# A planner's transfer time that grows with the bytes under way in front, in a four-layer graph network kernel

## The chip, the cores and the metric

The kernel runs on one core of one Trainium2 chip. The metric is the device time of one execution in microseconds (us), as the median of several runs; lower is better. The core has TensorE (matmuls; the profile shows them as PE, and the loading of their weights as PEld), VectorE (DVE), ScalarE (ACT), GpSimd (POOL) and SyncE (SP), which issues nearly all transfers here. The engines run side by side, each takes its instructions strictly in the order in which they were built, and they wait for each other through semaphores.

## The reference

Sixteen graphs of 1024 nodes with 128 features pass through four residual layers. `adj` is a sparse symmetric pattern with random weights, about 16 entries in a row.

```python
h = relu(layernorm(x)); x = x + L0(h, adj)   # relu([h, (adj^T h) / degree] W^T + b)
h = relu(layernorm(x)); x = x + L1(h, adj)   # leaky_relu((adj / degree) h W^T + b)
h = relu(layernorm(x)); x = x + L2(h, adj)   # two rounds of edge scores, see below
h = relu(layernorm(x)); x = x + L3(h, adj)   # attention over adj's entries: softmax((Wh1 + Wh2^T) * (adj + I)) Wh, elu
# L2, each of two rounds l:
score[n, m] = sigmoid(we2 . relu(a[n] + b[m] + be1) + be2)      # a, b: x times the halves of We1
msg = (adj * score) @ x
x = layernorm(x + relu([x, msg] Wu1 + bu1) Wu2 + bu2) * gamma + beta
```

## The kernel before

**Stages and lanes.** Three generators of work are woven by `weave` (L1630): `main` of graph b (both rounds of layer 2), `last` of graph b - 1 (end of layer 2, layer 3) and `first` of graph b + 1 (layers 0 and 1, then `build`). They belong to the lanes `m`, `c` and `a`, with buffers and PSUM banks of their own; lane `a` has a single bank while all three run. What repeats is one graph, about 290 us.

**Layer 2 on the sparse entries.** A graph's adjacency is cut in 128 x 128 tiles. `build` makes of each tile short lists of its entries: `pr`/`rank`, `on`, `onT`, `omT`, `om` are made one after another through lane `a`'s single bank, by TensorE matmuls (`pr`, `pn`, `pq`, `pm`) that ScalarE or VectorE read out at once. `twice` (L1116) copies `on` to `st` by four small transfers. `split` (L1211) turns the projected features (`bb` in PSUM) into two half-precision parts, `part`, and four transfers put them in a second arrangement, `both`. In a round, `gather` adds for each list the terms of both ends in PSUM (`pre`: two matmuls with `part`, two with `both`), `hid` is its relu, `dots` gives the scores `sc`, `scores` spreads them as `val`, `scatter` puts them back on the tile's grid (`p`, partly with 64-column matmuls), `upd` multiplies with the adjacency that `load_adj` fetched as `adj`, and `messages` sums `msg`.

**Between the rounds.** `between` (L1523) runs for each half of the nodes: it loads the transposed features `xm` by `self.back(xT, oldT)` (L1006), scales the messages into the same tile, and computes `h2` (TensorE row `h`, L594), `xn`, `tx` and the layer norm; it transposes the result (`tp`, read out as `xfT`), stores it (`xTk`), and calls `split` for the second round. The second round's first `pre` needs the first half's `both`.

**Layers 0 and 1.** `first` loads each row tile of `adj` twice (`at`, `ct`, 512 KB each), transposes it (`tn`), and stores it in `adjT`. `layer1` (L572) loads strips `l` of `adjT` (512 KB) into three row buffers, so that strip t waits until the matmuls `nb` of strip t - 3 are done. Layer 3 loads strips `a` (384 or 256 KB) into one buffer, each after VectorE's last use of the strip before.

**What sets the order.** All instructions are recorded first. `Issue` (L67) then plans them and fixes each engine's order by `settle` (L286), which ties neighbours in the plan together. `links` finds what an operation needs; `costs` (L131) gives each operation the time that its engine is busy and the time until its result is there (`late`); `walk` (L194) is a list scheduler: forward it goes through time, and at each point starts on the queue that can go first the ready operation of the best rank; it also keeps count of buffers and of at most eight transfers under way. `order` (L271) takes a first forward walk, then three times a backward walk, whose times give the ranks, and a forward walk with these ranks; it keeps the plan that ends first. All transfers but some of the weights' stand on SP's queue. A change of the matmul's form (float32 to other, 64 columns to full) costs the plan `SWITCH_NS`.

In `walk`, a transfer starts when the eighth before it has landed, and lands after its `late`, whatever else is under way.

Of the kernel before, what the change touches and what calls it, by code (L numbers as in the profile page):

```python
# [59 lines left out]
SIGNAL_NS = 45.0  # L60
RESULT_NS = {"PE": 163.0, "Activation": 120.0, "DVE": 88.0, "Pool": 80.0}
SWITCH_NS = 60.0
DMA_NS, DMA_NS_PER_BYTE, DMAS = 1900.0, 5.2e-3, 8
PASSES = 3


class Issue:  # L67
# [63 lines left out]
    def costs(self):  # L131


        self.busy, self.late, self.form = [], [], []
        for op, queue, kind in zip(self.ops, self.queue, self.kind):
            out, form = op.outs[0].bass_ap, (False, False)
            n, late = self.size(op.outs[0]), RESULT_NS.get(queue, 0.0)
            aps = [a.bass_ap for a in op.ins if hasattr(a, "bass_ap")]
            psum = bool(aps) and aps[0].space == bass.MemoryType.PSUM
            if kind == "Matmult":  # L140
                n = self.size(op.ins[0])
                form = op.ins[0].dtype == F32, out.shape[0] < 128
                if form[0]:
                    busy = max(n / 1.2 + 6, 112) * (1 if op.is_transpose else 2)
                else:
                    busy = 32 if form[1] else max(n / 2.4 + 2.5, 25)
            elif kind == "DMACopy":
                size = n * WIDTH[op.outs[0].dtype] * out.shape[0]
                inside = all(a.space == bass.MemoryType.SB for a in (out, aps[0]))
                busy = 630 if inside else 470  # L150
                late = DMA_NS + size * DMA_NS_PER_BYTE - busy
            elif queue == "Activation":
                busy = n / 1.2 + (50 if psum else 92) + 92 * (len(aps) - 1)
            elif queue == "DVE":
                wide = [a for a in aps if a.size() > 128]
                fast = kind == "TensorScalarPtr" and len(wide) == 1 and not psum
                if kind in ("BNStats", "TensorReduce"):
                    n = self.size(op.ins[0])
                busy = n * (0.53 if fast else 1.0625) + 55 + 64 * (len(aps) > len(wide))
            else:  # L160
                busy = 1560
            self.busy.append(busy)
            self.late.append(busy + late)
            self.form.append(form)
# [29 lines left out]
    def walk(self, rank, seq, back=False):  # L194


        n, queues = len(self.ops), sorted(set(self.queue))
        edges, others = (self.front, self.after) if back else (self.after, self.front)
        waits = [len(v) for v in others]
        users, turn, homes = self.turns(seq)  # L200
        given, parked, live, over = dict.fromkeys(homes, 0), {}, {}, {}
        ready, start, line = [0.0] * n, [0.0] * n, {q: [] for q in queues}
        soon, now = {q: [] for q in queues}, {q: [] for q in queues}
        free, landed, sent, was = dict.fromkeys(queues, 0.0), [0.0] * DMAS, 0, (False, False)

        def offer(j):

            new = {}
            for name in self.uses[j]:
                if name in turn and name not in live:  # L210
                    new.setdefault(self.tiles[name].tag, set()).add(turn[name])
                else:
                    ready[j] = max(ready[j], live.get(name, 0.0))
            for tag, mine in new.items():
                at = given[tag]
                while at in mine:
                    at += 1
                if at <= max(mine) or len(homes[tag]) < len(mine):
                    key = at + 1 if at <= max(mine) else given[tag]
                    parked.setdefault((tag, key), []).append(j)  # L220
                    return
                ready[j] = max(ready[j], sorted(homes[tag])[len(mine) - 1])
            heappush(soon[self.queue[j]], (ready[j], rank[j], j))

        for j in range(n):
            if not waits[j]:
                offer(j)
        for _ in range(n):
            at, q = min(
                (free[q] if now[q] else max(free[q], soon[q][0][0]), q)  # L230
                for q in queues if now[q] or soon[q]
            )
            while soon[q] and soon[q][0][0] <= at:
                heappush(now[q], heappop(soon[q])[1:])
            j = heappop(now[q])[1]
            if self.kind[j] == "DMACopy" and not back:
                at = max(at, landed[sent % DMAS])
                landed[sent % DMAS] = at + self.late[j]
                sent += 1
            elif q == "PE":  # L240
                at += SWITCH_NS * self.switched(j, was, back)
                was = self.form[j]
            start[j], free[q] = at, at + self.busy[j]
            line[q].append(j)
            end = at + (self.busy[j] if back else self.late[j] + SIGNAL_NS)
            freed = {}
            for name in self.uses[j]:
                users[name] -= 1
                over[name] = max(over.get(name, 0.0), end)
                if name not in turn:  # L250
                    continue
                tag = self.tiles[name].tag
                if name not in live:
                    live[name] = heappop(homes[tag])
                    freed.setdefault(tag, []).append(given[tag] + 1)
                    given[tag] += 1
                if not users[name]:
                    heappush(homes[tag], over[name])
                    freed.setdefault(tag, []).append(given[tag])
            for tag, keys in freed.items():  # L260
                for key in dict.fromkeys(keys):
                    for k in parked.pop((tag, key), ()):
                        offer(k)
            for k, lag in edges[j]:
                ready[k] = max(ready[k], at + lag)
                waits[k] -= 1
                if not waits[k]:
                    offer(k)
        return start, line
# [1545 lines left out]
```

## Time and profile before

| | |
|---|---|
| median of 3 runs | 4826.11 us (4824.32 to 4826.47) |
| the profiled execution | 4815.52 us |
| its span, first to last instruction | 4813.6 us |
| mean granted TensorE clock | 0.975 of full |
| transfers issued on SP | 4,418, of which 2,304 of 11 or 16 KB |
| moved | 618.15 MB, mean 128 GB/s |

The profile is one execution. A group's line reads: source line, engine, operation, output and inputs with their shapes, count, then busy time in us, mean ns of one, and the idle time of its engine just before such instructions with what ended most of it. A line of waits gives who waited for what: total us, times, longest. A line of transfers gives the count, the size of one and the median us from issue to landing. A timeline's line gives start, length and, in brackets, the idle time before it and what ended it. Names are without buffer numbers.

### The profile page before, as it was taken

The page shows a single profiled execution, that of the slowest core. Times are in us where ns is not written, and L with a number is a line of the kernel's source. Part 1 is how long each engine was busy: PE and PEld are TensorE (multiplying, and loading weights), DVE is VectorE, ACT ScalarE, POOL GpSimd, SP SyncE. Part 2 cuts the span into 40 slices and gives each one's busy share as a digit, 9 for nine tenths or more (in the row PEclk, how much of TensorE's full clock was granted, in tenths as well). Part 3 has the DMA queues.
Part 4 walks back from the last instruction along what each step waited for, and adds up shares of the span by engine and source line. Part 5 has one row for each costly group of instructions (what it writes and reads, how often), then busy time and mean ns, then how long its engine had stood idle before and what let it go on. Part 6 is the DMA issues. An engine that isn't in the chain of part 4 may idle for free.

```text
span 4813.6 us, 133882 instructions
## 1 busy us (share of the span) xinstructions
PE 4428.3 (92%) x53685; PEld 3601.4 (75%) x53685; DVE 3881.1 (81%) x9128; ACT 2982.1 (62%) x7238; POOL 175.2 (4%) x137
## 2 busy tenths in 40 slices
PE   6997999999999999999999999999999999999986
PEld 5776777777787777777777787777877777777765
DVE  3875797897978879797897978879797886978877
ACT  4756576575766657566575765757566575765643
POOL 0000000000000000000000000000000000000000
PEclk8997999999999999999999999999999999999997
DMA  7362535436354453635436354453535536354321
GB/s 208 79 186 69 161 100 159 122 91 197 83 170 113 129 162 86 180 96 155 133 85 191 95 162 122 114 173 93 173 102 149 141 85 181 99 158 122 81 74 57
DMA packets 945031, 618.15 MB, mean 128 GB/s; under 512 B 220688, under 2 KB 874768, under 8 KB 944400
## 3 DMA queue, kind: packets, MB, share of 16 engines
q1 hardware_dynamic: 939296, 607.87, 44.1%
q8 instruction: 423, 6.93, 0.6%
q10 hardware_dynamic: 5104, 1.65, 0.1%
q14 instruction: 208, 1.70, 0.1%
HBM read 446.44 MB, written 100.66 MB: 114 GB/s over the span
## 4 chain that ended last, share of the span: by engine, by line
PE 42%; DVE 25%; DMA 14%; ACT 10%; SPq 4%; issue 4%; POOL 0%; DVEq 0%; ACTq 0%; POOLq 0%
PE pre L1343 6%; DVE hid L1365 5%; PE p L1486 5%; PE nb L540 5%; DVE val L1441 4%; DMA at<-in_adj_dram 4%; PE msg L436 4%; PE sc L1389 4%; PE pre L1349 3%; PE h L594 3%; PE bb L548 2%; SPq L1123 2%; PE hp L436 2%; ACT hid L1364 2%; DMA both<-part 2%
## 5 line engine op out<-in xcount | busy, mean ns | idle before, releaser
L1365 DVE SCALAR_TENSOR_TENSOR hid<-pre,hid 128x320 f16<-128x320 f32 (+1 forms) x2048 | 996.4, 508 | 192.5 <-ACT hid L1364 184.8
L1364 ACT ACTIVATE hid<-pre 128x320 f16<-128x320 f32 (+1 forms) x2048 | 890.6, 458 | 365.4 <-PE pre L1349 355.5
L1343 PE MATMUL pre<-om,part 128*128 128x320 fp8e4 (+1 forms) x4096 | 968.6, 309 | 21.7 <-DVE hid L1365 9.8
L1349 PE MATMUL pre<-st,both 128*128 128x176 fp8e4 (+1 forms) x4096 | 692.0, 245 | 47.4 <-DMA both<-part 46.0
L1441 DVE TENSOR_TENSOR val<-onT,u 128x1024 f32<-128x1024 fp8e4 x576 | 697.8, 1220 | 3.3
L436 PE MATMUL msg<-upd,xf 128*128 128x128 f32 (+3 forms) x3008 | 648.6, 328 | 9.8 <-DVE upd L1493 9.8
L1349 PEld LDWEIGHTS <-both 128*128 128x128 f16 x4096 | 389.4, 98 | 208.0 <-issue 62.9
L1389 PE MATMUL sc<-slide,hid 128*128 128x1 f16 x12800 | 431.8, 163 | 19.1 <-DVE hid L1365 17.8
L436 PEld LDWEIGHTS msg<-upd,xf 128*128 128x128 f32 x3008 | 420.7, 191 | 30.0 <-DVE upd L1493 13.0
L1389 PEld LDWEIGHTS <-hid 128*128 128x128 f16 x12800 | 405.6, 96 | 49.8 <-DVE hid L1365 33.5
L1204 ACT ACTIVATE om<-pm 128x320 fp8e4<-128x320 f32 (+1 forms) x576 | 268.8, 467 | 231.5 <-PE pm L1150 225.7
L1486 PE MATMUL p<-val,omT 128*128 128x64 f16 (+1 forms) x6528 | 391.4, 204 | 16.7 <-DVE val L1441 15.1
L1410 ACT ACTIVATE tan<-sc,be_s,down 128x8 f32<-128x8 f32 (+1 forms) x960 | 296.4, 356 | 170.3 <-PE sc L1389 160.1
L1343 PEld LDWEIGHTS <-part 128*128 128x128 f16 x4096 | 345.8, 98 | 72.6 <-issue 45.3
L1493 DVE SCALAR_TENSOR_TENSOR upd<-p,adj 128x512 f32<-128x512 f32 x512 | 351.7, 687 | 28.8 <-PE p L1486 27.4
L1486 PEld LDWEIGHTS <-omT 128*128 128x128 fp8e4 x6528 | 337.4, 97 | 40.4 <-issue 25.1
L436 PE MATMUL hp<-wh,e 128*128 128x129 f32 x2048 | 323.8, 287 | 14.1 <-DVE e L768 13.9
L1107 ACT ACTIVATE far<-iota_off,mid 128x384 f16<-128x384 f16 x448 | 279.0, 627 | 56.6 <-DVE on L1111 45.5
L1197 DVE TENSOR_TENSOR omT<-pq,odd_off 128x384 fp8e4<-128x384 f32 x448 | 248.0, 554 | 64.0 <-PE pq L1193 62.0
L594 PE MATMUL h<-xm,wu_sb 128*128 128x512 f32 x512 | 274.3, 637 | 27.2 <-DMA xm<-xT 23.8
L1189 ACT ACTIVATE onT<-pn 128x256 fp8e4<-128x256 f32 (+1 forms) x576 | 250.7, 435 | 66.2 <-PE pn L1135 60.4
L436 PEld LDWEIGHTS hp<-wh,e 128*128 128x128 f32 x2048 | 273.2, 196 | 21.5 <-DVE e L768 17.2
(224 smaller groups left out, 7841.3 us busy)
## 6 DMA issues: line engine op xcount, KB each, us to landing
at<-in_adj_dram SPq DMA_DIRECT2D x128, 512.0 KB, 5.4
ct<-in_adj_dram SPq DMA_DIRECT2D x128, 512.0 KB, 5.4
adjT<-tn SPq DMA_DIRECT2D x128, 512.0 KB, 6.3
l<-adjT SPq DMA_DIRECT2D x128, 512.0 KB, 4.9
adj<-adjT SPq DMA_DIRECT2D x256, 256.0 KB, 3.5
a<-adjT SPq DMA_DIRECT2D x128, 384.0 KB, 3.7
both<-part SPq DMA_DIRECT2D x256, 128.0 KB, 2.3
adj<-adjT SPq DMA_DIRECT2D x448, 64.0 KB, 2.6
```

The source lines that it names most:

```text
L436: nc.tensor.matmul(dst, left, right, start=opened is None, stop=True, skip_group_check=True)
L594: nc.tensor.matmul(ps, wu1_sb[:, l, i, kb * P : (kb + 1) * P], src, start=(i == 0), stop=(i == 1),)
L1107: nc.scalar.activation(far[:, :n], self.iota[t == u][:, :n], AF.Abs, bias=s.mid[:, i : i + 1])
L1343: nc.tensor.matmul(pre[:, :c], parts[:, k, u % Q, 1 - d], om, start=(k == 0), stop=True, skip_group_check=True,)
L1349: ins = nc.tensor.matmul(pre[:, at : at + n], both[:, k, t % Q, d], st[:, k * n : (k + 1) * n], start=False, stop=True, skip_group_check=True,
L1364: nc.scalar.activation(hid[:, 0, :c], pre[:, :c], AF.Relu)
L1365: nc.vector.scalar_tensor_tensor(hid[:, 1, :c], pre[:, :c], 0.0, hid[:, 0, :c], op0=OP.max, op1=OP.subtract)
L1389: nc.tensor.matmul(sc[:, k, g : g + 1], self.hid[self.done + g][:, v, at : at + P], sign, start=(g, v, k) == (*order[0], 0), stop=True, sk ...
L1410: nc.scalar.activation(dst, src, AF.Tanh, bias=path.be2[:, self.l : self.l + 1], scale=path.down[:, self.l : self.l + 1],)
L1441: nc.vector.tensor_tensor(val, onT[:, i : i + each].rearrange("p i (c n) -> p i c n", n=n), v.rearrange("p k i o -> p i k o").to_broadcast ...
L1486: nc.tensor.matmul(dst, left, right, start=n < first, stop=True, skip_group_check=True)
L1493: nc.vector.scalar_tensor_tensor(upd, ps, S_SCALE, self.adj[:, d * Q : (d + 1) * Q], op0=OP.add, op1=OP.mult,)
```

## The change

A transfer's time in the plan had been 1900 ns plus 0.0052 ns for each byte. Now it is 1900 ns plus 0.0039 ns for each byte, plus 0.0033 ns for each byte that is still under way at its issue: of each of the last eight transfers, the share that has not landed, taken as linear in time. The added time counts for the landing (so for the limit of eight), for the release of buffers and for the operations that wait for the data. It is in the forward walk alone; the backward walk, which ranks, has each transfer's own time. No computation and no transfer is changed; the order of the instructions on the engines is what can differ.

```diff
-DMA_NS, DMA_NS_PER_BYTE, DMAS = 1900.0, 5.2e-3, 8
+DMA_NS, DMA_NS_PER_BYTE, DMA_NS_BEHIND, DMAS = 1900.0, 3.9e-3, 3.3e-3, 8
...
-        self.busy, self.late, self.form = [], [], []
+        self.busy, self.late, self.form, self.bytes = [], [], [], []
...
-            n, late = self.size(op.outs[0]), RESULT_NS.get(queue, 0.0)
+            n, late, size = self.size(op.outs[0]), RESULT_NS.get(queue, 0.0), 0
...
+            self.bytes.append(size)
...
-        free, landed, sent, was = dict.fromkeys(queues, 0.0), [0.0] * DMAS, 0, (False, False)
+        free, sent, was = dict.fromkeys(queues, 0.0), [(0.0, 0.0, 0)] * DMAS, (False, False)
...
+            more = 0.0
             if self.kind[j] == "DMACopy" and not back:
-                at = max(at, landed[sent % DMAS])
-                landed[sent % DMAS] = at + self.late[j]
-                sent += 1
+                at = max(at, sent[0][1])
+                more = DMA_NS_BEHIND * sum(
+                    n * (end - at) / (end - then) for then, end, n in sent if end > at
+                )
+                sent = sent[1:] + [(at, at + self.late[j] + more, self.bytes[j])]
...
-            end = at + (self.busy[j] if back else self.late[j] + SIGNAL_NS)
+            end = at + (self.busy[j] if back else self.late[j] + more + SIGNAL_NS)
...
-                ready[k] = max(ready[k], at + lag)
+                ready[k] = max(ready[k], at + lag + more * (lag > 0.0))
```

## The prediction

> **What bounds the kernel now.** I read the page from the top: busy time of each engine, then the costliest groups, then the time to landing of each transfer, then who waited for whom on TensorE, then the same for the SP queue, and last the timeline of one batch round the two largest waits that a transfer ends.
>
> ```profile
> PE 4428.3 (92%) x53685; PEld 3601.4 (75%) x53685; DVE 3881.1 (81%) x9128; ACT 2982.1 (62%) x7238; POOL 175.2 (4%) x137
> ...
> L1486 PE MATMUL p<-omT,val 128*64 128x128 fp8e4 x5376 | 238.0, 224 | 14.2 <-DVE upd L1493 13.9
> ```
>
> TensorE is the bound: its matmul row stands idle for 4813.6 - 4428.3 = 385 us. Batches 5 to 9 (1450 to 2900 us) idle 87 us, or 17 us in each batch of 290. So at most some 8% is to be won, and only what changes TensorE's own waits or its own work counts. The second line is kept for later: matmuls on a 64-column share of the array.
>
> ```profile
> at<-in_adj_dram SPq DMA_DIRECT2D x128, 512.0 KB, 5.4
> adjT<-tn SPq DMA_DIRECT2D x128, 512.0 KB, 6.3
> both<-part SPq DMA_DIRECT2D x256, 128.0 KB, 2.3
> st<-on SPq DMA_DIRECT2D x1792, 11.0 KB, 1.8
> xm<-xT SPq DMA_DIRECT2D x32, 256.0 KB, 5.2
> xm<-xTk SPq DMA_DIRECT2D x32, 256.0 KB, 3.3
> ```
>
> Two rows of 256 KB, one landing in 5.2 us and one in 3.3: size alone doesn't set the time. The old formula (1900 ns + 0.0052 ns a byte) gives 3.26 us for both. I fitted all SP transfers of this trace to their own bytes and to the bytes under way at their issue: 1859 ns + 0.00387 ns a byte + 0.00329 ns a byte in front. The old formula is off by 1.05 us rms and 0.48 us short on average, the new one by 0.55 us and 0.05. So the new planner sees transfers about as they are.
>
> ```profile
> PE pre L1349 <- DMA both<-part: 46.0, 46, 2.4
> PE pm L1150 <- DVE omT L1197: 24.6, 42, 1.3
> PE h L594 <- DMA xm<-xT: 23.8, 14, 2.7
> PE tn L1035 <- ACT tn L1036: 17.7, 28, 1.7
> PE tn L1035 <- DVE own L565: 12.3, 13, 1.9
> PE tn L1035 <- DMA at<-in_adj_dram: 10.5, 19, 1.4
> ```
>
> The columns are total us, times, longest. Where matmul and weight-load row are idle together, the xm wait counts 18.8 us and the both wait 30.1 us; 22.5 of the latter fall on one place, the first `pre` of the second round, 14 times at 1.6 us. The xm wait is also one place in each batch, 1.7 us. These are the waits that a better guess of landing times can remove.
>
> ```profile
> 1439.26 0.36 SPq L972 DMA_DIRECT2D l<-adjT  x1
> 1439.67 0.57 SPq L1006 DMA_DIRECT2D xm<-xT  x1
> ...
> 1442.54 1.06 PE L540 MATMUL nb<-z,l 128*128 128x128 f32 x8
> 1446.23 1.10 PE L594 MATMUL h<-xm,wu_sb 128*128 128x512 f32 x2 [2.63 <-DMA xm<-xT]
> ...
> 1452.87 0.59 SPq L1228 DMA_DIRECT2D both<-part  x1
> ...
> 1457.55 0.49 PE L1349 MATMUL pre<-st,both 128*128 128x256 fp8e4 x3 [2.27 <-DMA both<-part]
> ```
>
> The xm load is issued right behind a 512 KB strip l, which itself waits until `nb` of three strips before frees its row (at 1439.2); it lands after 6.4 us. The old planner put 4.8 us of matmuls between that `nb` and the `h` that reads xm. Needed: 0.4 (issue of l) + 6.4 + 0.1 = 6.9 us. The wait is the planner's error.
>
> **What the Trainium skill says.** "DMA: Bandwidth & Descriptors", section "Queues, rings and completion order": each DMA engine takes a ring's descriptors in order, so a transfer stands behind the bytes issued before it. The trace agrees (5.2 against 3.3 us above). The same page, "Anatomy of one DMA", fits about 2.0 us + bytes/436e3, which is 3.2 us for 512 KB; here such loads take 5.4, and the measurement decides. "TensorEngine Tiling (Array Packing)", "Key Properties": changing the tiling mode drains TensorE. The trace agrees: by the starts of neighbouring matmuls without a wait, the one before a run of 64-column matmuls takes 90 ns more than usual, and the last of the run 156 ns against 29 within it. A run costs 90 + 127 = 217 ns over its matmuls; the planner counts 60. "Perfetto Trace Analysis", "Identifying the Most-Contended Engine", warns that matmul busy time is no measure of headroom; so I count waits and changed work, not busy shares.
>
> **The change, part by part.** No instruction is added or removed; each engine gets the same ones in another order (POOL's is the same). The backward pass, which ranks, has only the shorter own time (512 KB: 4.6 us before, 3.9 now), so loads rank as less urgent, while the forward pass sees them land later. What comes of both stands in the two built orders; I compare these, and price the matmuls between two places by the mean distance of such matmuls in this trace.
>
> 1. The xm load. Between the freeing `nb` and `h` there are now 30 matmuls instead of 20, worth 7.6 us instead of 4.8; a strip load `a`, which waits for VectorE, no longer stands in front of it on SP. 7.6 covers 6.9. Gain: the 18.8 us in which both rows were idle, nearly all: -19.
> 2. both, second round, first half. From the last `bb` to the first `pre` that reads it: 5.6 us of matmuls before, 7.0 now. Needed by the sample above: 1457.55 - 1449.94 (end of that `bb`) = 7.6; by the mean wait (5.6 + 1.6) 7.2. A 384 KB `a` load moves from ahead of it to behind it. Left over 0.2 us x 14 = 3 of 22.5: -19.
> 3. The other `both` places: first round 5.1 us of cover to 5.7, second half 4.7 to 7.2. Their waits are 6.6 us ended by the DMA and about 5 shown as issue; gain -8.
> 4. The transposes `tn` of the adjacency tiles: `at` now has some 1.5 us more work in front of it. Counting for every read-out by ScalarE or VectorE how far the matmuls up to the next reader, or to the next user of its single PSUM bank, fall short of its duration, `tn` goes from 47 to 26 us. The sum of this count over all read-outs is 299 us before, and the trace has 308 us of idle time ended by ScalarE and VectorE: the count has the right size. I take -15 of the 21, since the three wait rows hold only 40 us.
> 5. The builder's single bank by the same count: `om` 85 to 90, `onT` 52 to 66, `rank` 12 to 20, `omT` 53 to 36: +11. `xfT` 8 to 14, `hT` +2.5, `upd` -4, the layer outputs -5: together +10.
> 6. Narrow runs. The order splits the 5,376 narrow matmuls into 528 runs instead of 428. 100 x 217 ns = +22. Float32 to other changes go from 2,026 to 2,038 at 4 ns each: nothing.
> 7. SP's queue. It has no spare order: a strip load `a` blocks it while it waits for VectorE, up to 34.7 us at a time (440 us in all). Loads of `a` move behind xm and both, the copies `st` and loads `adj` change places with them; nine in ten of those keep over 10 us of matmuls as cover, against 1.8 to 4.5 us of landing. New waits are not shown by the trace: bound from 0 to 20 us (one of 1.4 us per batch, like those removed), nearer the bottom: +6. Below nothing isn't likely, since all named gains are counted.
>
> Sum: -19 - 19 - 8 - 15 + 10 + 22 + 6 = -23. Start and end of the program (57 us idle in the first 290, 72 in the last 464) keep their chains. The profiled execution took 4815.5 us (span 4813.6), the median of the runs is 4826.1, 10.6 more; against its own time this makes 4792, against the median 4803. Since every removed wait brings the next one nearer, I take some 3 off: **4806 us**.
>
> **Rivals.** *Half of the gain comes back.* The need in step 2 is 7.6 rather than 7.2, the longer landings move with the reordered loads, and steps 1 to 4 bring 35 instead of 61: -35 + 38 = +3, within 0.2%. For: TensorE is in order, a wait taken away is often found again one instruction later. Against: the two places are fixed points of each batch, and their cover grows by 2.9 and 1.4 us in 14 batches. Time 4818 to 4834. *The change doesn't reach the places that wait*: excluded in the main by the two orders; it would give 4826 and belongs to this case. *The narrow runs decide.* The planner moves scatter matmuls one by one into the gaps that it now sees, and prices a mode change at 60 ns where the trace shows 217. The place is the scatter `p` of all 16 batches; the price is 22 us for certain, and with the builder's +10 and SP's 6 to 20 up to 52. It decides as soon as the waits bring less than 28 us; if they bring 20, the sum is +18 to +32: about 4850. For it: the count of runs is a fact of the order. Against: the waits to be won add up to over 60. *A gain beyond the sum*: all of steps 1 to 4 and nothing new, 4780.
>
> **How the numbers follow.** Some 0.2% (10 us) is about what a measurement of this kernel can tell from no change. The forecast 0.47 and the gain beyond the sum 0.10: faster, 4775 to 4816, 0.57. Half of the gain comes back, or the change doesn't reach the waits: within 0.2%, 4816 to 4836, 0.21. The narrow runs decide: slower, 4836 to 4865, 0.22. The forecast's own range is 4785 to 4816; the range asked for leaves out the fastest tenth and the slowest: 4782 to 4846.
>
> **What would show it.** Right: the wait of `h` for xm (23.8 us) nearly gone; that of `pre` for both (46.0) at 20 or less; the `tn` waits smaller; the narrow `p` group with an unchanged count, but TensorE's busy time up by some 20 us. Wrong: both rows still there or turned into waits for another load (`l`, `a`); the idle time of TensorE unchanged at 385; or busy time up by 40, which would make it slower.

## The result, and the profile after

The changed kernel takes 4797.72 us (median of 4 runs, 4792.57 to 4802.62) against 4826.29 for the kernel before in the same runs: a ratio of 0.9938, with a 95% interval of 0.9921 to 0.9956. The profiled execution has a span of 4790.7 us, 22.9 below that of before. All line numbers in the changed file are 4 higher.

The page's first part after the change:

```profile
PE 4448.1 (93%) x53685; PEld 3602.2 (75%) x53685; DVE 3884.2 (81%) x9128; ACT 3003.7 (63%) x7238; POOL 180.8 (4%) x137
```

The group of 64-column matmuls in it, from the groups with shapes kept apart (busy us and mean ns, then the idle time before them):

```profile
L1490 PE MATMUL p<-omT,val 128*64 128x128 fp8e4 x5376 | 257.3, 224 | 1.9 <-DVE upd L1497 1.8
```

TensorE is busy 19.8 us longer and idle 4790.7 - 4448.1 = 342.6 us instead of 385.3: 42.7 less. The same 5,376 narrow (64-column) matmuls take 257.3 us instead of 238.0. A group's busy time overlaps that of its neighbours, and other groups moved both ways, so the two rises of about 20 us are not the same thing; the section on the prediction comes back to this.

Whom TensorE's matmuls waited for (total us, times, longest):

```profile
PE tp L1538 <- DVE xf L626: 34.2, 15, 2.7
...
PE pre L1353 <- DMA both<-part: 22.9, 27, 2.0
...
PE pm L1154 <- DVE omT L1201: 13.5, 28, 1.5
...
PE tn L1039 <- DMA at<-in_adj_dram: 4.1, 4, 2.0
...
PE tn L1039 <- ACT tn L1040: 2.6, 12, 0.6
...
PE h L598 <- DMA xm<-xT: 0.5, 1, 0.5
```

The wait for xm fell from 23.8 to 0.5 us, that for both from 46.0 to 22.9, the three `tn` waits from 40.5 to 6.7. On top stands the wait of the transposes `tp` for the layer norm's result, once in a batch, 2.3 us each on average. Before, it was nearly nothing:

```profile
PE tp L1534 <- DVE xf L622: 2.7, 14, 0.2
```

The batch of the forecast's sample, now (start, length, what; timeline of SP and TensorE):

```profile
1433.11 0.38 SPq L976 DMA_DIRECT2D l<-adjT  x1
1433.54 0.57 SPq L1010 DMA_DIRECT2D xm<-xT  x1
...
1440.22 1.02 PE L598 MATMUL h<-xm,wu_sb 128*128 128x512 f32 x2
...
1446.47 0.38 PE L1353 MATMUL pre<-st,both 128*128 128x256 fp8e4 x2 [0.74 <-DMA both<-part]
```

The xm load is still issued right behind a strip l, but it lands 5.2 us after its issue and `h` comes after 6.7 us, with no wait before it; what stood 2.27 us before the first `pre` that reads both is 0.74 us.

### The profile page after: what moved, and what is told of

It is laid out like the page before. It is cut to its first block, busy times and chain, and to the rows that moved or that the text cites. A ratio compares the mean times of both kernels' runs of the same rounds, so it can differ in the third digit from the quotient of the medians.

```text
span 4790.7 us, 133931 instructions
## 1 busy us (share of the span) xinstructions
PE 4448.1 (93%) x53685; PEld 3602.2 (75%) x53685; DVE 3884.2 (81%) x9128; ACT 3003.7 (63%) x7238; POOL 180.8 (4%) x137
## 4 chain that ended last, share of the span: by engine, by line
PE 54%; DVE 22%; DMA 11%; ACT 5%; SPq 3%; issue 3%; POOL 0%; DVEq 0%; ACTq 0%; POOLq 0%
PE nb L544 7%; PE pre L1347 7%; PE p L1490 7%; DVE hid L1369 5%; PE msg L440 5%; PE sc L1393 4%; PE bb L552 4%; PE pre L1353 4%; DMA a<-adjT 3%; PE h L598 3%; DVE val L1445 2%; SPq L1127 2%; DVE omT L1201 2%; PE tn L1039 2%; PE xn L607 2%
## 5 line engine op out<-in xcount | busy, mean ns | idle before, releaser
L1368 ACT ACTIVATE hid<-pre 128x320 f16<-128x320 f32 (+1 forms) x2048 | 900.6, 459 | 308.0 <-PE pre L1353 294.6
L1353 PE MATMUL pre<-st,both 128*128 128x176 fp8e4 (+1 forms) x4096 | 679.1, 244 | 23.5 <-DMA both<-part 22.9
L440 PE MATMUL msg<-upd,xf 128*128 128x128 f32 (+3 forms) x3008 | 660.8, 330 | 20.9 <-DVE upd L1497 19.8
L1490 PE MATMUL p<-val,omT 128*128 128x64 f16 (+1 forms) x6528 | 401.2, 206 | 17.1 <-DVE val L1445 17.1
L1347 PEld LDWEIGHTS <-part 128*128 128x128 f16 x4096 | 339.0, 98 | 75.5 <-issue 46.7
L1490 PEld LDWEIGHTS <-omT 128*128 128x128 fp8e4 x6528 | 345.3, 98 | 42.0 <-issue 26.4
L544 PE MATMUL nb<-z,ct 128*128 128x128 f32 x2048 | 262.8, 280 | 10.4 <-DMA ct<-in_adj_dram 7.1
```

The costliest lines, as they stand in the source:

```text
L440: nc.tensor.matmul(dst, left, right, start=opened is None, stop=True, skip_group_check=True)
L544: nc.tensor.matmul(ps, mat[:, k], z[:, k], start=(k == 0), stop=(k == T - 1))
L1347: nc.tensor.matmul(pre[:, :c], parts[:, k, u % Q, 1 - d], om, start=(k == 0), stop=True, skip_group_check=True,)
L1353: ins = nc.tensor.matmul(pre[:, at : at + n], both[:, k, t % Q, d], st[:, k * n : (k + 1) * n], start=False, stop=True, skip_group_check=True,
L1368: nc.scalar.activation(hid[:, 0, :c], pre[:, :c], AF.Relu)
L1490: nc.tensor.matmul(dst, left, right, start=n < first, stop=True, skip_group_check=True)
```

## The experiments

**The theories.** *Forecast*: the planner now knows the landing behind other bytes, so the two waits go, and what the order costs elsewhere is added. *Mean error*: landings were planned 0.48 us too early on average; any formula that is right on average does the same. *Draw*: a list scheduler's order changes all over with any constant, so 0.6% may be luck.

Each run is compared with the kernel before on the same chip; the ratios, not the times, are comparable with the first result (before was 4814 to 4815 us in these). All runs stand in the order of their ratio. Error is planned minus measured landing, over the 4,418 SP transfers of the trace before. The idle and busy times are TensorE's matmul row in the profiled execution; the columns xm and both are the time in which matmul and weight-load row stood idle at the `h` that reads xm and at the first `pre` of the second round, whatever ended it. The clock is the mean granted TensorE clock of an execution, as the median of the run's executions, not of the profiled one alone.

| run | mean error, rms (ns) | ratio (interval) | idle | busy | narrow runs | xm | both | clock |
|---|---|---|---|---|---|---|---|---|
| e9, changed + keep narrow | +48, 545 | 0.9910 (0.9890 to 0.9930) | 371 | 4405 | 225 | 0.1 | 33.0 | 0.974 |
| r4, changed, 3.4 for 3.3 | +69, 548 | 0.9929 (0.9910 to 0.9949) | 333 | 4427 | 439 | 0.1 | 10.4 | 0.970 |
| e3, constant 2380 | +2, 934 | 0.9933 (0.9912 to 0.9954) | 321 | 4449 | 489 | 0.8 | 6.6 | 0.972 |
| **changed** | +48, 545 | 0.9938 (0.9921 to 0.9956) | 343 | 4448 | 528 | 0.5 | 14.5 | 0.972 |
| e2, behind alone | +226, 636 | 0.9946 (0.9929 to 0.9963) | 353 | 4444 | 389 | 0.0 | 7.1 | 0.971 |
| s1, changed, old ranks | +48, 545 | 0.9950 (0.9934 to 0.9967) | 349 | 4431 | 484 | 0.8 | 10.3 | 0.973 |
| **before** | -478, 1049 | 1 | 385 | 4428 | 428 | 23.3 | 27.2 | 0.975 |
| e4, slope 5.3 for 5.2 | -464, 1041 | 1.0002 (0.9994 to 1.0010) | 370 | 4453 | 461 | 9.3 | 10.4 | 0.975 |
| r1, changed, constant 1370 | -482, 726 | 1.0011 (1.0000 to 1.0023) | 375 | 4444 | 452 | 1.9 | 26.4 | 0.972 |
| s2, constant 2390 | +12, 934 | 1.0016 (1.0006 to 1.0026) | 332 | 4482 | 528 | 0.0 | 6.8 | 0.968 |
| e7, behind for xm and both alone | not one value | 1.0083 (1.0059 to 1.0107) | 372 | 4474 | 478 | 0.6 | 3.0 | 0.969 |
| r2, slope 3.9, constant 2680 | +123, 996 | 1.0101 (1.0084 to 1.0118) | 404 | 4477 | 457 | 3.5 | 22.3 | 0.970 |
| r3, constant 2860 | +482, 1051 | 1.0129 (1.0113 to 1.0146) | 410 | 4463 | 498 | 3.2 | 29.0 | 0.970 |
| e1, slope 3.9 alone | -657, 1186 | 1.0138 (1.0117 to 1.0158) | 410 | 4478 | 491 | 0.3 | 5.7 | 0.971 |

### One part alone: the slope

```diff
-DMA_NS, DMA_NS_PER_BYTE, DMAS = 1900.0, 5.2e-3, 8
+DMA_NS, DMA_NS_PER_BYTE, DMAS = 1900.0, 3.9e-3, 8
```

> The old formula with the new slope (0.0039 ns a byte) and nothing for the bytes in front. The built order has 5.0 us of matmuls ahead of the h that reads xm (needed 6.9), 6.0 ahead of the first pre of the second round (needed 7.2 to 7.6) and 491 narrow runs (428 before). Theory of the forecast (the bytes in front are what matters): both waits stay, together 30 to 40 us with both rows idle, TensorE's busy time up by 63 x 0.217 = 14 us, time 1.000 of before, from 0.998 to 1.005. Rival 'smaller own time is enough': 0.994 like the full change. Rival 'any other constant gives another draw of the order': anywhere from 0.994 to 1.006, with no relation to the two waits.

Measured 1.0138: slower than every theory's range, the draw's (0.994 to 1.006) too. The two waits are gone nevertheless (0.3 and 5.7 us). TensorE's longest waits in this kernel:

```profile
PE tn L1035 <- DVE own L565: 38.9, 26, 4.0
...
PE p L1486 <- DVE val L1441: 26.6, 47, 2.6
PE nb L540 <- DVE o L581: 24.6, 21, 2.5
PE tp L1534 <- DVE xf L622: 24.0, 16, 2.4
PE sc L1389 <- DVE hid L1365: 23.9, 33, 2.0
```

The time has gone into waits for VectorE. Added up over the matmul row, the waits that a transfer ends fell from 96 to 46 us, and those that VectorE or ScalarE ends rose from 262 to 342. So an order without the two waits isn't for that reason a faster one. The forecast's theory, in the form "these waits are the gain", is hit by this run.

### One part alone: the bytes in front

```diff
-DMA_NS, DMA_NS_PER_BYTE, DMA_NS_BEHIND, DMAS = 1900.0, 3.9e-3, 3.3e-3, 8
+DMA_NS, DMA_NS_PER_BYTE, DMA_NS_BEHIND, DMAS = 1900.0, 5.2e-3, 3.3e-3, 8
```

> The term for the bytes in front alone, with the old slope of 0.0052 ns a byte, so that landings are planned too late on average. Cover of xm 6.6 us with no strip l right in front, cover of both 7.2, 389 narrow runs. Theory of the forecast: the two waits fall from 41 to below 8 us, TensorE's busy time falls by 39 x 0.217 = 8 us, time 0.991 of before (0.988 to 0.995). Rival 'the smaller slope makes the gain': 1.000 or slower.

Measured 0.9946, both waits at 7.1 us in all. The new term alone gives the gain, and the new slope alone a loss; the intervals of this run and of the whole change overlap. Busy time did not fall by 8 us; it rose by 16, in a profile whose mean granted clock was 0.968 against 0.975 before.

### Longer for all, without the queue, twice

```diff
-DMA_NS, DMA_NS_PER_BYTE, DMAS = 1900.0, 5.2e-3, 8
+DMA_NS, DMA_NS_PER_BYTE, DMAS = 2380.0, 5.2e-3, 8
```

> The old formula with its constant raised from 1900 to 2380 ns, which takes away its mean error of 0.48 us but knows nothing of the queue. Covers 4.6 and 6.1 us, 489 narrow runs, and the read-outs of PSUM fall 20 us shorter of their durations than before. Theory of the forecast: the both wait stays in the main (15 to 22 us), busy time up 13 us, time 1.004 of before (1.000 to 1.008). Rival 'longer landings on average are enough': 0.994 to 0.996.

> The old formula with a constant of 2390 ns: a second draw of the run with 2380, which came out at 0.993 although it knows nothing of the queue. 528 narrow runs instead of 489 (+8 us). Theory 'right on average is enough': 0.994 to 0.996. Theory 'the first draw was lucky' (two blind plans with landings as late or later gave 1.010 and 1.013): 1.000 to 1.012.

Measured 0.9933 with 2380 ns and 1.0016 with 2390. The first looked like the end of the forecast's theory: a formula that knows nothing of the queue does as well. The second, 10 ns further, shows that the same formula can also gain nothing; which of the two is the lucky draw, two runs can't tell. The idle time is the same within 12 us, the busy time 33 us longer. Of that, 39 narrow runs are some 8 us by the price of 217 ns. The mean granted clock of the two profiles was 0.973 and 0.969; 0.4% of the busy time is 18 us, an estimate that takes all of it to go with the clock.

One thing speaks for the blind formula: e3 and s2 have less idle time (321 and 332 us) than the changed kernel (343). What made s2 slow is its busy time.

### Two nudges: how far the draw goes

```diff
-DMA_NS, DMA_NS_PER_BYTE, DMAS = 1900.0, 5.2e-3, 8
+DMA_NS, DMA_NS_PER_BYTE, DMAS = 1900.0, 5.3e-3, 8
```

> The old formula with its slope moved from 0.0052 to 0.0053 ns a byte: a change with no meaning, to see how far the order's draw alone moves the time. Cover of both 5.7 us, 461 narrow runs (busy time +7 us), read-outs 26 us less short. Theory of the forecast: the both wait stays at some 20 us, time 0.996 of before (0.993 to 1.000). Rival 'another draw': anything up to 0.6% either way; if it reaches 0.994, the gain of the change can't be told from a draw by its time alone, only by its waits.

```diff
-DMA_NS, DMA_NS_PER_BYTE, DMA_NS_BEHIND, DMAS = 1900.0, 3.9e-3, 3.3e-3, 8
+DMA_NS, DMA_NS_PER_BYTE, DMA_NS_BEHIND, DMAS = 1900.0, 3.9e-3, 3.4e-3, 8
```

> The changed formula with 0.0034 instead of 0.0033 ns for each byte in front: another draw with the same meaning. 439 narrow runs instead of 528. Theory 'the formula decides': 0.994, within 0.3%. Theory 'a draw': anywhere. If a narrow run costs 217 ns beside the rest, TensorE's busy time is 19 us below that of the changed kernel and the ratio 0.990.

Measured 1.0002 for the old formula and 0.9929 for the new one: each within 0.1% of its neighbour, in spite of 89 narrow runs less in the second. In its profile the busy time is 21 us below the changed kernel's, as 89 x 0.217 = 19 us would have it; the ratio, though, moved by 0.0009 (4 us) only, within the intervals. The profiled execution of r4 was the fastest of its four, 15 us below their median, so its profile flatters it.

### Right on average, or knowing the queue

```diff
-DMA_NS, DMA_NS_PER_BYTE, DMA_NS_BEHIND, DMAS = 1900.0, 3.9e-3, 3.3e-3, 8
+DMA_NS, DMA_NS_PER_BYTE, DMA_NS_BEHIND, DMAS = 1370.0, 3.9e-3, 3.3e-3, 8
```

> The changed formula, bytes in front and all, with its constant lowered from 1900 to 1370 ns, so that a landing is planned 0.48 us too early on average, as before the change (by the transfers of the trace before: mean -482 ns, rms 726). Theory 'the mean error decides' (planned minus measured: slope alone -657 ns and 1.014; before -478 and 1.000; constant 2380 +2 and 0.993; changed +48 and 0.994; behind alone +226 and 0.995): 1.000, from 0.997 to 1.004. Theory 'knowing the queue decides': 0.994 to 0.996. Theory 'a draw of the order': anywhere from 0.990 to 1.014.

```diff
-DMA_NS, DMA_NS_PER_BYTE, DMAS = 1900.0, 5.2e-3, 8
+DMA_NS, DMA_NS_PER_BYTE, DMAS = 2680.0, 3.9e-3, 8
```

> Nothing for the bytes in front, the new slope of 0.0039 ns a byte, and a constant of 2680 ns: right on average (+123 ns), wrong one by one (rms 996), and 0.71 us too early for transfers of 512 KB. Theory 'the mean error decides': 0.994 (0.990 to 0.997), against 1.014 with the constant of 1900. Theory 'the landing of the 512 KB loads decides' (slope alone -1.49 us and 1.014, before -0.81 and 1.000, changed +0.05 and 0.994): 0.998 to 1.001. Theory 'knowing the queue decides': 1.000 or slower. Draw: anywhere.

```diff
-DMA_NS, DMA_NS_PER_BYTE, DMAS = 1900.0, 5.2e-3, 8
+DMA_NS, DMA_NS_PER_BYTE, DMAS = 2860.0, 5.2e-3, 8
```

> The old formula with a constant of 2860 ns: landings planned 0.48 us too late on average, 512 KB loads 0.15 us. Theory 'the mean error decides', with a plan that is too late costing as little as behind alone (+226 ns and 0.995): 0.995 to 0.999, since work is held back that could start. Theory 'later is always better': 0.990 to 0.993. Theory 'a draw': anywhere from 0.990 to 1.014.

Measured 1.0011, 1.0101 and 1.0129. The first is what the mean-error theory asked for: with the queue known but all landings 0.48 us early, nothing is won, and the wait at both is back at 26.4 us. The second speaks against it: right on average, and still 1% slower. It is not right for each size, though: it plans loads of 512 KB 0.71 us too early, e3 only 0.33 us, and no run separates that from not knowing the queue. The third says that too late isn't safe either. The four plans that know the queue and are right on average (changed, r4, s1, e2), so that single landings are off by 545 to 636 ns rms, all lie between 0.9929 and 0.9950. The eight formulas with 726 ns or more lie between 0.9933 and 1.0138, and seven of them at 1 or above. That is a pattern, not a proof: by idle time alone, the two plans that are right on average to 12 ns and blind to the queue, e3 and s2, are the best of all.

### The two transfers alone

```diff
+                if not self.uses[j] or not any(u.startswith(("xm_", "both_")) for u in self.uses[j]):
+                    more = 0.0
                 sent = sent[1:] + [(at, at + self.late[j] + more, self.bytes[j])]
```

(The slope is 5.2e-3, so all other transfers keep the old formula.)

> The old formula, with 0.0033 ns for each byte in front added for the transfers into xm and both alone: the two waits of the forecast and nothing else. Cover of xm 6.6 us, of both 7.2, 478 narrow runs (+50, +11 us), read-outs as short as before. Theory of the forecast (the two waits are the gain): both waits below 10 us together, 0.993 to 0.996. Theory 'all landings have to be planned right, these two are a small part': 0.998 to 1.004. Draw: anywhere.

Measured 1.0083. Both waits are gone (3.6 us together), and the kernel is slower. TensorE's longest waits here:

```profile
PE pm L1156 <- DVE omT L1203: 46.7, 66, 3.1
PE pre L1349 <- DVE hid L1371: 32.1, 53, 2.8
...
PE tp L1540 <- DVE xf L628: 28.0, 14, 2.6
...
PE h L600 <- DMA xm<-xTk: 15.4, 14, 2.7
```

The builder's chain waits 46.7 us for `omT`, where it was 24.6, and `h` in the lane `last` now waits for its own load. Even so, all idle time together is 14 us below that of before. It is the busy time that makes this kernel slow: 46 us above that of before, with 50 narrow runs more (11 us) and a clock of 0.969 in all but one of its four executions, against 0.975. Correcting the two places alone isn't enough.

### The ranks

```diff
-                self.front[j].append((k, lag + self.busy[j] - self.busy[k]))
+                rank = 1.3e-3 * self.bytes[k] * done
+                self.front[j].append((k, lag + rank + self.busy[j] - self.busy[k]))
```

> The changed kernel's forward walk, but the ranking backward walk counts 0.0052 ns a byte as before the change. Cover of xm 8.4 us, of both 6.5, 484 narrow runs (-44, -9 us against the changed kernel). Theory 'the landings of the forward walk make the gain': 0.992 (0.990 to 0.996). Theory 'the lower rank of loads makes it': 1.000 or slower.

Measured 0.9950. The backward walk may count the old time; with the landings of the forward walk alone, most of the gain is there, and the intervals of the two overlap.

### Narrow matmuls kept together

```diff
-            j = heappop(now[q])[1]
+            j = None
+            if q == "PE" and was[1] and not back:
+                j = min((v for v in now[q] if self.form[v[1]][1]), default=None)
+            if j is None:
+                j = heappop(now[q])[1]
+            else:
+                now[q].remove(j)
+                heapify(now[q])
+                j = j[1]
```

> The changed kernel's planner with one more rule: after a narrow matmul, a ready narrow one goes first. 225 narrow runs instead of 528. If a run costs 214 ns (86 before it, 128 after its last), TensorE's busy time falls by 303 x 0.214 = 65 us to some 4385; if the waits stay, 0.980 of before (0.976 to 0.986). If the price is only apparent (covered by waits that come anyway), busy time falls and idle time grows by as much: 0.994.

The first part of this kernel's page:

```profile
PE 4405.4 (92%) x53685; PEld 3581.9 (75%) x53685; DVE 3876.1 (81%) x9128; ACT 3013.1 (63%) x7238; POOL 200.2 (4%) x137
```

Its group of narrow matmuls, with shapes kept apart:

```profile
L1498 PE MATMUL p<-omT,val 128*64 128x128 fp8e4 x5376 | 193.8, 222 | 1.5 <-DVE upd L1505 1.0
```

Two of TensorE's waits in it:

```profile
...
PE p L1498 <- DVE val L1453: 35.4, 53, 2.9
PE pre L1361 <- DMA both<-part: 32.1, 15, 2.8
```

The narrow group falls from 257.3 to 193.8 us with 303 runs less: 0.210 us each. From before to after it had risen by 19.3 for 100 runs: 0.193. As proof of the price this is weak, since the modelled end of each run's last matmul overlaps its neighbours. All busy time decides (over all fourteen profiles it gives 0.20 us a run, see below): it falls by 42.7 us, not by 65, and idle time grows by 28. In this pair two thirds of the price came through, and two thirds of what came was taken back by waits (the first `pre` of the second round alone stands 33 us, after 14.5). Measured 0.9910, short of the 0.980 expected. It is the lowest ratio of all; its interval overlaps that of the change, so that it beats the kernel before is shown, that it beats the changed one is not.

## Why the prediction was right

It said 4806 us, its own case 4785 to 4816; 4797.7 is in it. The two parts of its sum held: less waiting by 45 and more work by 22, against 42.7 and 19.8 in the two profiles. How they came about is another matter. Step by step, with idle times of both rows unless said otherwise:

| step | said | measured |
|---|---|---|
| 1. xm | -19 | 23.3 to 0.5 |
| 2. both, second round | -19 | 27.2 to 14.5 |
| 3. the other both places | -8 | first round 12.7 to 6.3; second half 6.1 to 2.9 |
| 4. `tn` (matmul row) | -15 | 40.5 to 6.7 |
| 5. builder's bank and the rest | +10 | `om` 35.2 to 48.5, `onT` 13.9 to 18.0, `omT` 35.3 to 24.0, `xfT` 4.3 to 9.4 |
| 6. narrow runs | +22 | the narrow group's busy time +19.3 |
| 7. new waits | +6, from 0 to 20 | `tp` after `xf` alone 2.5 to 33.8, outside its bound |

Steps 1 and 3 came as worked out, or a little better. The prediction's 18.8 and 30.1 us for the two waits, and the 22.5 at the one place, were counted too low: it went by what the weight load's own semaphores show. In the trace each of the 14 `h` starts about 0.1 us after xm lands, and ScalarE's share of xm had been ready 1.3 to 2.8 us before the wait ended, so all 23.3 us belong to the transfer; in the same way all 46.0 us at `both` end with a landing. Step 2 brought 13 us of the 19: nearly all that stays at that place still waits for `both`. Step 4 was sized too small: the count had said 21, and I took 15 with the three rows of 40 us as a ceiling. Step 5 is +11 over the four named groups. Step 7 was wrong in place and size: I looked on SP's queue, and the new wait came on VectorE. In one half of most batches TensorE had 8.9 us of matmuls between `tx` and `tp` before, and 6.6 after. The layer norm between them, a chain of VectorE instructions and one on GpSimd, ended 9.4 and 9.2 us after `tx`, so `tp` now waits 2.65 us. The count of read-outs could not see it, since it takes one instruction at a time between two TensorE places. The error of step 7 (31 against 6) and that of step 4 (34 against 15) nearly cancel, and that is luck.

Step 6 had luck too. Busy time does not go with the narrow runs alone: in the traces TensorE's clock is full or half, and at half clock the same matmuls take longer. It stood at half for 238 us of the profile of before and 266 us of that after, which is 14 us of full-speed work lost. A straight-line fit of the busy time of all fourteen profiles to the number of narrow runs and to 1/clock gives 0.20 us for a run (standard error 0.04) and a busy time that grows about in step with 1/clock, with 10 us rms left over. By it 100 runs and the lower clock make +35, and the measured +19.8 lies 15 below.

What the experiments take from the prediction is the reason it gave first. It read the gain from two waits first; e1, s2 and e7 lose both and gain nothing, and in e9 and r1 one is back whole. Any new order seems to move them: the waits of the matmul row that a transfer ends fall in every run, from 96 us to between 24 and 71. What VectorE and ScalarE end tells the runs apart better: 262 us before, 270 after, 267 to 301 in the other runs below 1, but 342, 330 and 332 in e1, r2 and r3; the four near 1 or a little above (e4, r1, s2, e7) have 269 to 299 and can't be told apart by it. So the gain goes with the whole plan. That it needs landings planned right one by one fits most of the runs but isn't shown. Its second rival, that the narrow runs decide, had about the right price (0.20 us by the fit, 0.217 said), but the effect was too small to decide. Its first, that half of the gain comes back, did not come for the change; it came for e9.

The count of shortfalls seemed to match the trace of before (299 against 308 us). But the 308 held the xm wait of 18.8 us and other waits that end with a landing; without them it is 276. Nor is the count a forecast for another order: for e3 it gives 319, 20 more than before, and the trace has 278, 2 more.

Open stays how much of 0.6% is the formula and how much the draw. Four plans with the good formula between 0.9929 and 0.9950, and one of eight others below 1, make luck alone unlikely; but e3 shows that a blind formula can draw the same, and no run tells which of the many changed places carries the gain.

The granted clock moves with the plan too, but it does not make the gain: it is 0.972 after against 0.975 before, and the changed kernel and e1 have nearly the same clock at 0.9938 and 1.0138. For e7 and s2, with 0.969 and 0.968, the fit makes it some 28 us of e7's 40 and more than all of s2's 8. The traces show where it comes from. From 290 to 4350 us the fourteen profiles have 378 stretches at half clock, most of them 3.4 or 6.8 us long. In the 3.4 us before such a stretch TensorE was idle for 1.8 us at the median; of 3.4 us taken anywhere, one in twenty has more than 1.2 us of idle time. So waits that stand close together seem to cost more than their own length: in the profile after, 8 of the 13 long waits of `tp` are followed within 4 us by a stretch at half clock. That the idle time brings on the half clock is read from this order in time; no run changed the one alone. Neither the prediction nor the planner counts this.

## What to carry to other kernels

When a planner fixes the order, fit its transfer times on the trace one by one, with the bytes in front, and look at the spread of the error as well as its mean: here all four plans with both small were faster than before, and of the eight other formulas one, a blind one. A plan with both small is the safer choice, not a proven cause. Before believing a gain of half a per cent from a planner's constant, run its neighbours: 2380 and 2390 ns differed by 0.8%. A wait that disappears in the new trace is not yet the reason for the gain; sum idle and busy time of the bounding engine, look for the new wait in the chains that the edit didn't name, and check the granted clock before busy time is put down to the work.

## What the runs showed of the hardware

A change between full and 64-column matmuls costs TensorE about 0.20 us of busy time for each run of narrow ones (standard error 0.04), by the fit over fourteen orders with 225 to 528 runs. From the matmuls' starts it is some 90 to 100 ns before the run and some 128 after it in all fourteen profiles. The planner counts 60.

A transfer on SP's queue landed after 1859 ns + 0.00387 ns for each byte of its own + 0.00329 ns for each byte under way in front, over 4,418 transfers, with 0.55 us rms left over; without the last term it is 0.93.

With the same instructions in another order, the mean granted clock was 0.964 to 0.971 in twenty executions of s2 and 0.972 to 0.978 in 23 of the kernel before on the same chip. In the traces it is full or half, and the half-clock stretches follow 3.4 us in which TensorE was idle for about half the time, though no single wait from 290 to 4350 us of the profile of before was over 2.7 us.
